# Queries, keys, values and tail contexts of the last attention in four column tiles

## The chip, the cores and the metric

The kernel runs on one core of one Trainium2 chip. The metric is the device time of one execution in microseconds (us). Before the change three runs gave 2605.72, 2614.56 and 2616.25 us; the median is 2614.56. In the profiles, PE is TensorE (matmuls), PEld its loading of the stationary side, DVE is VectorE, ACT is ScalarE, POOL is GpSimd, and SP issues most of the DMAs.

## The reference

Four layers follow each other, each added to its input: a self-attention with 8 heads, a causal convolution, a GRU over 256 steps, and a second attention with 16 heads of 16 channels over 256 channels and 512 positions, for 16 batches. All of it is float32. Only the last one is touched:

```python
def proj(W):
    y = jnp.einsum('oc,bct->bto', W, x)
    return y.reshape(B, T, H, Dh).transpose(0, 2, 1, 3)
Q, K, V = (proj(Wq), proj(Wk), proj(Wv))
att = jnp.einsum('bhqd,bhkd->bhqk', Q, K) * (1.0 / math.sqrt(Dh))
att = att + b[0]
m = mask[:, None, None, :]
att = att * m + (1.0 - m) * NEG_INF
att = jax.nn.softmax(att, axis=-1)
y = jnp.einsum('bhqk,bhkd->bhqd', att, V)
```

The mask is drawn with a chance of about one half, so about half of the 512 positions of a batch are keys that count.

## The kernel before

The program runs the first attention, then the convolution and the recurrence together, then the last attention (`attend_together`, from L1251). This form of the last attention is used when the keys that count fit into 320 places (`ROOM`) in every batch; they do here. The kept rows of a batch are first gathered into a table in DRAM and read back (`send`, `fetch_table`), so that scores and contexts are computed for 320 keys in place of 512: two chunks of 128 and a tail of 64.

**A batch.** `gather` transposes the kept rows (L1323) and the batch's x (L1338) on PE, and makes the values: for each of three key chunks a matmul of the kept rows with the value weights (L1351). `heads` makes queries and keys for half of the heads at a time (L1381). `group` then works on one of four groups; a group takes every other head of one half, four heads, each in 32 of the 128 partitions. It computes scores with queries in the rows for the maximum over keys (L1415 for the two chunks, L1421 for the tail), which DVE takes (L1430, L1435, L1442). The maxima are transposed on PE (L1448) and added to the queries (L1451), so that the second scores (L1461), with keys in the rows, come out shifted; ACT exponentiates them (L1468). `weigh` multiplies these with the values (L1475 for chunks, L1479 for the tail) and adds the chunks in one bank, which ACT copies out (L1488). `finish` sends the sums to DRAM, inverts them on DVE, spreads them, and scales and adds on POOL (L1516 to L1524) before the output goes out.

**Tile shapes on PE.** The profile names a matmul's tile as rows*columns of the array that it occupies. A float32 matmul of the code shows as two MATMUL rows, and each is called a pass here. Steps of this stage come in five shapes: 128*128 (transposes and the products L1351 and L1381); 32*128, four row tiles abreast (L1415, L1461 for the chunks); 64*128, two row tiles (L1421, L1461 for the tail); 128*32, four column tiles abreast (L1475); and 128*64, two column tiles (L1479). The recurrence and its input products (L1063, L1075, L1084) use 128*32 throughout. Passes that run abreast are called a wave.

The tail holds 64 keys, but its score is laid out so that the 128 partitions hold two heads' tail keys each, 64 and 64. The tail's values (`V3`) therefore have zeros for the other head in each half.

**Who sets the order.** The last attention is not written in the order in which it runs. Each step is put into a `Plan` (L168) with an engine, a duration, a due time, what it depends on and which buffers it takes. `Plan.order` then simulates the engines and picks, among the steps that can start, the one that is due first. A step on PE has a mode beside it; a step of the mode that ran last is treated as due 0.25 earlier (`STAY`), and one of another mode is taken to cost 0.2 more (`SWITCH`). Steps without a mode, the transposes and products, count as one mode of their own. The result is a fixed order for each engine, and each engine runs its own in sequence.

Buffers that matter here: three pairs of score banks (`pairs`), one small bank for transposes and products (`banks`), one bank for contexts (`accs`), three for exponentials (`es_`).

Of the kernel before, what the change touches and what calls it, by code (L numbers as in the profile page):

```python
# [16 lines left out]
P = 128  # L17
NEG = -1e30
B, D, T = 16, 256, 512
# [4 lines left out]
H3, DK3, R3 = 16, 16, 32  # L24
# [226 lines left out]
def tile_kernel(ctx: ExitStack, tc: tile.TileContext, x, cond, Wq0, Wo0, W_ih, W_hh, b_ih, b_hh,  # L251
                Wq3, Wk3, Wv3, b3, consts, out, cols):
    nc = tc.nc
# [997 lines left out]
    def attend_together():  # L1251
# [3 lines left out]
        with ExitStack() as es:  # L1255
# [37 lines left out]
            for i in range(2):  # L1293
# [4 lines left out]
                        nc.gpsimd.memset(V3[i][64 * odd : 64 * odd + 64, :, q, odd::2, e : e + 1], 1.0)  # L1298
                nc.gpsimd.memset(NM[i], 0.0)

            def gather(b, g0):

                ub, mk, t, xk, x3, v = us.new(), mks.new(), ts_.new(), xks.new(), x3s.new(), vs.new()
                n = plan.add("DVE", 0.4, g0 - 4, [us.take(ub)], lambda: nc.vector.tensor_scalar(
                    UB[ub.i], cst("iota"), keysT[:, b : b + 1], NEG, ALU.is_ge, ALU.mult))
                for q in range(2):
                    n = plan.add("DVE", 0.4, g0 - 4, [n] + ([mks.take(mk)] if q == 0 else []), lambda q=q: nc.vector.tensor_scalar(
                        MK[mk.i][:, q], UB[ub.i], cst(f"oneC{q}"), top[:, q : q + 1], ALU.mult, ALU.add))
                us.free(ub, n)
                made = n  # L1310
                sent = [plan.add("POOL", 1.2, g0 - 7, ahead[-3:-2], lambda f=f: send(b, f)) for f in range(NT)]
                landed = plan.add("LAG", 2.0, g0 - 7, sent, lambda: None)
                got = []
                for c0 in (0, 2):
                    got.append(plan.add("SP", 3.0, g0 - 6, [landed] + (got or [ts_.take(t)]), lambda c0=c0: fetch_table(b, c0, XS[t.i])))
                moved, turned = [], []
                for kc in range(KC):
                    sm = banks.new()

                    def turn(kc=kc, sm=sm):  # L1320
                        for c in range(NK):
                            r = P if c < 2 else TAILK
                            nc.tensor.transpose(SM[sm.i][:, c * P : c * P + r], XS[t.i][0:r, c, kc * P : (kc + 1) * P], ident[0:r, 0:r])  # L1323
                    m = plan.add("PE", 0.35, g0 - 4.2 + 0.2 * kc, got + [banks.take(sm)] + ([xks.take(xk)] if kc == 0 else moved), turn)
                    c = plan.add("ACT", 0.5, g0 - 4.2, [m],
                                 lambda kc=kc, sm=sm: nc.scalar.copy(XK[xk.i][:, kc, 0:ROOM], SM[sm.i][:, 0:ROOM]))
                    c = plan.add("ACT", 0.3, g0 - 4.2, [c],
                                 lambda kc=kc, sm=sm: nc.scalar.copy(XK[xk.i][:, kc, ROOM:], SM[sm.i][:, 2 * P : ROOM]))
                    banks.free(sm, c)
                    moved.append(c)  # L1330
                ts_.free(t, m)
                ahead.append(m)
                for kc in range(KC):
                    sm = banks.new()

                    def turn(kc=kc, sm=sm):
                        for j in range(NT):
                            nc.tensor.transpose(SM[sm.i][:, j * P : (j + 1) * P], xT[:, j, b, kc * P : (kc + 1) * P], ident)  # L1338
                    m = plan.add("PE", 0.45, g0 - 3.6 + 0.2 * kc, [banks.take(sm)] + ([x3s.take(x3)] if kc == 0 else turned), turn)
                    c = plan.add("DVE", 0.7, g0 - 3.6, [m], lambda kc=kc, sm=sm: nc.vector.tensor_copy(X3[x3.i][:, kc], SM[sm.i]))  # L1340
                    banks.free(sm, c)
                    turned.append(c)
                v_done = []
                for c0 in range(0, NK, 2):
                    sm = banks.new()
                    some = range(c0, min(c0 + 2, NK))

                    def values(some=some, sm=sm, c0=c0):
                        for c in some:
                            for kc in range(KC):  # L1350
                                nc.tensor.matmul(SM[sm.i][:, (c - c0) * D : (c - c0 + 1) * D],  # L1351
                                                 lhsT=XK[xk.i][:, kc, c * P : c * P + P], rhs=wv3T[:, kc],
                                                 start=(kc == 0), stop=(kc == KC - 1))
                    m = plan.add("PE", 0.86 * len(some), g0 - 1.6 + 0.2 * c0, moved + v_done + [banks.take(sm)] + ([] if c0 else [vs.take(v)]), values)
                    for c in some:
                        def spread(c=c, sm=sm, c0=c0):
                            src = SM[sm.i][:, (c - c0) * D : (c - c0 + 1) * D]
                            if c < 2:
                                dst = V[v.i][:, c].rearrange("p (h q) r -> p h (q r)", q=2).rearrange("p h (m i) -> p h m i", i=DK3)
                                nc.scalar.copy(dst[:, :, 0::3], src.rearrange("p (h m i) -> p h m i", m=2, i=DK3))  # L1360
                                return
                            src = src.rearrange("p (m s q i) -> p m s q i", m=2, q=2, i=DK3)
                            for q in range(2):
                                for odd in range(2):
                                    r = slice(64 * odd, 64 * odd + 64)
                                    nc.scalar.copy(V3[v.i][r, :, q, odd::2, DK3 * q : DK3 * q + DK3], src[r, :, odd::2, q])
                        m2 = plan.add("ACT", 0.4 if c < 2 else 1.0, g0 - 1.6, [m], spread)
                        v_done.append(m2)
                    banks.free(sm, m2)
                return mk, xk, x3, v, moved, turned, v_done, made, m  # L1370

            def heads(b, hp, g0, mk, xk, x3, moved, turned, made):
# [3 lines left out]
                for w, x_, X_, deps, name, n, dur in ((wq3T, x3, X3, turned, "q", T, 1.72), (wk3T, xk, XK, moved + [made], "k", ROOM, 1.1)):  # L1376
                    sm = banks.new()

                    def product(w=w, x_=x_, X_=X_, n=n, sm=sm):
                        for kc in range(KC):  # L1380
                            nc.tensor.matmul(SM[sm.i][:, 0:n], lhsT=w[:, kc, hp * P : (hp + 1) * P], rhs=X_[x_.i][:, kc, 0:n],  # L1381
                                             start=(kc == 0), stop=(kc == KC - 1))
                    m = plan.add("PE", dur, gp - 2.6 + 0.1 * (name == "k"), deps + [banks.take(sm)] + [(qs if name == "q" else ks).take(x) for x in (qt if name == "q" else kt)], product)
                    for q in range(2):
                        if name == "q":
                            c = plan.add("ACT", 0.7, gp - 2.6, [m], lambda q=q, sm=sm: nc.scalar.activation(
                                Q[qt[q].i], SM[sm.i], AF.Identity, bias=cst(f"oneC{q}"), scale=cst(f"scaleC{q}")))
                        else:
                            c = plan.add("DVE", 0.6, gp - 2.5, [m], lambda q=q, sm=sm: nc.vector.scalar_tensor_tensor(
                                K[kt[q].i][:, 0:ROOM], SM[sm.i][:, 0:ROOM], cst(f"headC{q}"), MK[mk.i][:, q], ALU.mult, ALU.add))  # L1390
                        done[q].append(c)
                    banks.free(sm, c)
# [10 lines left out]
            def group(g, b, gn, qt, kt, ready, v, v_done):  # L1403
# [50 lines left out]
                for kc in range(NK):  # L1454
# [17 lines left out]
                    def weigh(kc=kc, e=e):  # L1472
                        if kc < 2:
                            for j in range(J):
                                nc.tensor.matmul(AV[acc.i][R * j : R * j + R, :], lhsT=V[v.i][:, kc, 8 * (g // 2) + 2 * j + q],  # L1475
                                                 rhs=E[e.i][:, j], start=(kc == 0), stop=False)
                            return
                        for jp in range(2):
                            nc.tensor.matmul(AV[acc.i][2 * R * jp : 2 * R * jp + 2 * R, :],  # L1479
                                             lhsT=V3[v.i][:, g // 2, q, 2 * jp : 2 * jp + 2].rearrange("p s r -> p (s r)"),  # L1480
                                             rhs=E[e.i][:, jp], start=False, stop=True)
                    last = plan.add("PE", 0.88, gn + kc / NK + 0.2, done + v_done + ([accs.take(acc)] if kc == 0 else [last]), weigh,
                                    mode="c32" if kc < 2 else "c64")
                    es_.free(e, last)
                qs.free(qt, *scored)
                ks.free(kt, *scored)
# [90 lines left out]
```

## Time and profile before

| | us |
|---|---|
| runs before, median (lowest, highest) | 2614.56 (2605.72, 2616.25) |
| the profiled execution | 2617.86 |
| its span | 2616.1 |
| PE busy in the span | 2448.6 |
| DVE busy, ACT busy | 1780.2, 1016.1 |
| L1381 query products, x128 passes of 512 columns, busy | 65.3 |
| L1381 key products, x128 passes of 320 columns, busy | 44.2 |
| L1351 values, x192 passes of 256 columns, busy | 51.8 |
| L1475 contexts of chunks, x1024 passes of 512 columns, busy | 137.2 |
| L1479 contexts of the tail, x256 passes of 512 columns, busy | 69.0 |

The page gives shares of the whole span. The span has three stages with different limits: the first attention up to about 580 us, the recurrence up to about 1680, and the last attention to the end. "Busy" counts the time in which at least one instruction of a group runs, and passes run several abreast, so the busy time of a group divided by its count is not the duration of one. For what a step costs the engine, differences between the starts of neighbouring steps in the timeline are of more use.

### The profile page before, as it was taken

The page shows a single profiled execution, that of the slowest core. Times are in us where ns is not written, and L with a number is a line of the kernel's source. Part 1 is how long each engine was busy: PE and PEld are TensorE (multiplying, and loading weights), DVE is VectorE, ACT ScalarE, POOL GpSimd, SP SyncE. Part 2 cuts the span into 40 slices and gives each one's busy share as a digit, 9 for nine tenths or more (in the row PEclk, how much of TensorE's full clock was granted, in tenths as well). Part 3 has the DMA queues.
Part 4 walks back from the last instruction along what each step waited for, and adds up shares of the span by engine and source line. Part 5 has one row for each costly group of instructions (what it writes and reads, how often), then busy time and mean ns, then how long its engine had stood idle before and what let it go on. Part 6 is the DMA issues. An engine that isn't in the chain of part 4 may idle for free.

```text
span 2616.1 us, 100684 instructions
## 1 busy us (share of the span) xinstructions
PE 2448.6 (94%) x45506; PEld 1635.2 (63%) x45506; DVE 1780.2 (68%) x3810; ACT 1016.1 (39%) x2459; POOL 385.3 (15%) x382
## 2 busy tenths in 40 slices
PE   5999889959999999999999999789999999999995
PEld 3545444437888888888888888644444444444442
DVE  1578778866888888888888655455666566665652
ACT  2444444422333333333333332234444544555452
POOL 2333231210000000000000000132223222231113
PEclk9999999979999999999999999989999999999997
DMA  5222221130000000000000000010011100110001
GB/s 178 69 65 68 62 63 35 35 137 3 5 4 4 5 4 4 4 5 4 4 4 5 5 4 4 5 49 28 28 32 36 41 29 28 33 39 26 19 19 36
DMA packets 54738, 80.22 MB, mean 31 GB/s; under 512 B 15824, under 2 KB 33434, under 8 KB 54292
## 3 DMA queue, kind: packets, MB, share of 16 engines
q1 hardware_dynamic: 45076, 56.66, 7.1%
q0 software_dynamic: 9216, 16.96, 2.2%
q8 instruction: 360, 5.90, 1.0%
q14 instruction: 86, 0.70, 0.1%
HBM read 45.05 MB, written 36.75 MB: 31 GB/s over the span
## 4 chain that ended last, share of the span: by engine, by line
PE 80%; issue 6%; DMA 4%; DVE 4%; POOL 3%; ACT 1%; SPq 0%; POOLq 0%; another core or an unknown queue 0%; DVEq 0%; ACTq 0%
PE pr L1084 10%; PE pz L1084 9%; PE pn L1084 9%; PE sC L1461 8%; PE sC L1415 7%; PE avC L1475 5%; PE pt L1075 4%; PE pr L1063 4%; PE pz L1063 4%; PE smC L1381 4%; PE sC L1421 3%; PE avC L1479 2%; PE smA L908 2%; DMA backA<-result,goto 2%; PE smC L1351 2%
## 5 line engine op out<-in xcount | busy, mean ns | idle before, releaser
L1430 DVE TENSOR_REDUCE nmC<-sC 128x4 f32<-128x1024 f32 x256 | 301.8, 1221 | 208.5 <-PE sC L1415 206.8
L1468 ACT ACTIVATE wih<-sC 128x1024 f32<-128x1024 f32 x320 | 313.6, 1022 | 236.6 <-PE sC L1461 218.6
L1084 PE MATMUL pr<-whh,hist 128*32 128x128 f32 x8192 | 281.6, 275 | 14.2 <-DVE hist L1120 10.2
L1084 PEld LDWEIGHTS pr<-whh,hist 128*32 128x32 f32 x8192 | 218.8, 110 | 118.5 <-DVE hist L1120 51.1
L1084 PE MATMUL pz<-whh,hist 128*32 128x128 f32 x8192 | 279.6, 273 | 2.2 <-issue 2.2
L1084 PE MATMUL pn<-whh,hist 128*32 128x128 f32 x8192 | 278.9, 273 | 0.0
L533 DVE SCALAR_TENSOR_TENSOR yw<-xT,condT,yw 128x512 f32<-128x512 f32 x360 | 269.5, 749 | 6.8
L1063 PE MATMUL pr<-wih,xw 128*32 128x128 f32 x4096 | 222.6, 274 | 22.2 <-DMA wv3nat<-in_L_cond_Wv_dram 19.1
L1084 PEld LDWEIGHTS pz<-whh,hist 128*32 128x32 f32 x8192 | 237.3, 110 | 3.3 <-issue 3.0
L1084 PEld LDWEIGHTS pn<-whh,hist 128*32 128x32 f32 x8192 | 237.1, 110 | 0.1
L1461 PE MATMUL sC<-qC,kC 32*128 32x512 f32 (+1 forms) x1280 | 231.7, 632 | 0.4 <-ACT wih L1468 0.3
L1063 PE MATMUL pz<-wih,xw 128*32 128x128 f32 x4096 | 224.1, 274 | 3.7 <-issue 3.4
L1115 ACT ACTIVATE nn<-pre 128x64 f32<-128x64 f32 x256 | 65.7, 257 | 384.3 <-DVE pre L1113 377.0
L1108 ACT ACTIVATE r<-pr 128x128 f32<-128x128 f32 x256 | 71.0, 277 | 319.2 <-PE pr L1084 318.9
L881 DVE TENSOR_REDUCE whh<-smA 128x2 f32<-128x640 f32 (+2 forms) x211 | 150.2, 752 | 65.1 <-PE smA L873 46.2
L1415 PE MATMUL sC<-kC,qC 32*128 32x256 f32 x2048 | 185.5, 401 | 0.0
L297 POOL DMA_INDIRECT table<-xT,togo x128 | 133.5, 1043 | 248.2 <-DMA table<-xT,togo 169.4
L1516 POOL TENSOR_TENSOR aC<-aC,pbC 128x512 f32<-128x512 f32 x64 | 81.2, 1270 | 590.9 <-ACT wih L1468 287.7
L1075 PE MATMUL pt<-xw,wih 128*32 128x256 f32 x2048 | 166.8, 382 | 0.0
L1288 POOL MEMSET pbC<- 128x512 f32 x4 | 2.3, 625 | 1101.2 <-DVE xT L1092 1101.2
L1109 DVE STREAM_TRANSPOSE rT<-r 128x128 f32<-128x128 f32 x256 | 79.7, 311 | 118.8 <-ACT r L1108 102.4
L1415 PEld LDWEIGHTS sC<-kC,qC 32*128 32x128 f32 x2048 | 128.7, 184 | 46.2 <-issue 16.5
(178 smaller groups left out, 3853.8 us busy)
## 6 DMA issues: line engine op xcount, KB each, us to landing
xA<-in_x_dram SPq DMA_DIRECT2D x16, 512.0 KB
pbC<-sums SPq DMA_DIRECT2D x256, 32.0 KB
out_dram<-oC SPq DMA_DIRECT2D x32, 256.0 KB
table<-zeros SPq DMA_DIRECT2D x16, 320.0 KB
xsA<-table SPq DMA_DIRECT2D x16, 256.0 KB
result<-ocA SPq DMA_DIRECT2D x16, 256.0 KB
xsC<-table SPq DMA_DIRECT2D x16, 256.0 KB
wih<-in_L_cond_W_ih_dram SPq DMA_DIRECT2D x4, 768.0 KB
```

Of the source, the lines that this page charges most:

```text
L297: nc.gpsimd.indirect_dma_start(tables[b], bass.IndirectOffsetOnAxis(togo[:, f, b : b + 1], 0), xT[:, f, b], None, bounds_check=ROOM - 1, o ...
L533: nc.vector.scalar_tensor_tensor(acc, xT[:, f, :, lo : lo + WIN], condT[:, f, k : k + 1], xT[:, f, :, t0 : t0 + WIN] if k == 0 else acc, A ...
L881: nc.vector.tensor_reduce(dst[:, lo : lo + len(some)], SM[0:n, some[0] : some[-1] + 1, 0:ROOM], AX.X, ALU.max, negate=True)
L1063: nc.tensor.matmul(sets[k % 2][0 if g == GATE_R else 2][32 * j : 32 * j + 32].rearrange("p (f i) -> p f i", i=32), lhsT=x2, rhs=gates(wih, ...
L1075: nc.tensor.matmul(ps[32 * j : 32 * j + 32], lhsT=wih[:, kc, 2 * T + fo * P + 32 * j : 2 * T + fo * P + 32 * j + 32], rhs=parts[p][:, kc]. ...
L1084: nc.tensor.matmul(ps[32 * j : 32 * j + 32].rearrange("p (f i) -> p f i", i=32), lhsT=slot[:, f], rhs=gates(whh, f, j)[:, g], start=False, ...
L1381: nc.tensor.matmul(SM[sm.i][:, 0:n], lhsT=w[:, kc, hp * P : (hp + 1) * P], rhs=X_[x_.i][:, kc, 0:n], start=(kc == 0), stop=(kc == KC - 1))
L1415: nc.tensor.matmul(S[st[j // 2].i][:, j % 2, u * 2 * P : (u + 1) * 2 * P], lhsT=Q[qt.i][R * j : R * j + R, c : c + P], rhs=K[kt.i][R * j : ...
L1430: nc.vector.tensor_reduce(dst[:, :, :, e_at + 1], S[st[jp].i].rearrange("p j (u k) -> p j u k", u=2), AX.X, ALU.max, negate=True)
L1461: nc.tensor.matmul(S[st[j // 2].i][:, j % 2, :], lhsT=K[kt.i][r, kc * P : kc * P + P] if kc < 2 else K[kt.i][r, ROOM:], rhs=Q[qt.i][r, :], ...
L1468: lambda jp=jp, st=st, e=e: nc.scalar.activation(E[e.i][:, 2 * jp : 2 * jp + 2], S[st[jp].i], AF.Exp))
L1475: nc.tensor.matmul(AV[acc.i][R * j : R * j + R, :], lhsT=V[v.i][:, kc, 8 * (g // 2) + 2 * j + q], rhs=E[e.i][:, j], start=(kc == 0), stop= ...
```

## The change

Queries, keys and values are computed by four matmuls of 32 columns each in place of one of 128. A helper, `columns`, issues them, all with the same right side. The tail's contexts, so far two matmuls of 64 columns that each served two heads, become four of 32 columns. The plan's modes follow: products, values and tail contexts now carry the mode "c32" of the other contexts. The plan's durations and due times stay.

```diff
+            def columns(ps, left, right, kc):
+
+                for j in range(4):
+                    r = slice(R3 * j, R3 * j + R3)
+                    nc.tensor.matmul(ps[r], lhsT=left[:, r], rhs=right, start=(kc == 0), stop=(kc == KC - 1))
+
             def gather(b, g0):
...
                     def values(some=some, sm=sm, c0=c0):
                         for c in some:
                             for kc in range(KC):
-                                nc.tensor.matmul(SM[sm.i][:, (c - c0) * D : (c - c0 + 1) * D],
-                                                 lhsT=XK[xk.i][:, kc, c * P : c * P + P], rhs=wv3T[:, kc],
-                                                 start=(kc == 0), stop=(kc == KC - 1))
-                    m = plan.add("PE", 0.86 * len(some), g0 - 1.6 + 0.2 * c0, moved + v_done + [banks.take(sm)] + ([] if c0 else [vs.take(v)]), values)
+                                columns(SM[sm.i][:, (c - c0) * D : (c - c0 + 1) * D], XK[xk.i][:, kc, c * P : c * P + P], wv3T[:, kc], kc)
+                    m = plan.add("PE", 0.86 * len(some), g0 - 1.6 + 0.2 * c0, moved + v_done + [banks.take(sm)] + ([] if c0 else [vs.take(v)]), values, mode="c32")
...
                     def product(w=w, x_=x_, X_=X_, n=n, sm=sm):
                         for kc in range(KC):
-                            nc.tensor.matmul(SM[sm.i][:, 0:n], lhsT=w[:, kc, hp * P : (hp + 1) * P], rhs=X_[x_.i][:, kc, 0:n],
-                                             start=(kc == 0), stop=(kc == KC - 1))
-                    m = plan.add("PE", dur, gp - 2.6 + 0.1 * (name == "k"), deps + [banks.take(sm)] + [...], product)
+                            columns(SM[sm.i][:, 0:n], w[:, kc, hp * P : (hp + 1) * P], X_[x_.i][:, kc, 0:n], kc)
+                    m = plan.add("PE", dur, gp - 2.6 + 0.1 * (name == "k"), deps + [banks.take(sm)] + [...], product, mode="c32")
...
-                        for jp in range(2):
-                            nc.tensor.matmul(AV[acc.i][2 * R * jp : 2 * R * jp + 2 * R, :],
-                                             lhsT=V3[v.i][:, g // 2, q, 2 * jp : 2 * jp + 2].rearrange("p s r -> p (s r)"),
-                                             rhs=E[e.i][:, jp], start=False, stop=True)
+                        for j in range(J):
+                            nc.tensor.matmul(AV[acc.i][R * j : R * j + R, :], lhsT=V3[v.i][:, g // 2, q, j],
+                                             rhs=E[e.i][:, j // 2], start=False, stop=True)
                     last = plan.add("PE", 0.88, gn + kc / NK + 0.2, done + v_done + ([accs.take(acc)] if kc == 0 else [last]), weigh,
-                                    mode="c32" if kc < 2 else "c64")
+                                    mode="c32")
```

More of the change, by code (lines that the diff above doesn't have):

```diff
@@ L1380, in product @@
                         for kc in range(KC):
-                            nc.tensor.matmul(SM[sm.i][:, 0:n], lhsT=w[:, kc, hp * P : (hp + 1) * P], rhs=X_[x_.i][:, kc, 0:n],
-                                             start=(kc == 0), stop=(kc == KC - 1))
-                    m = plan.add("PE", dur, gp - 2.6 + 0.1 * (name == "k"), deps + [banks.take(sm)] + [(qs if name == "q" else ks).take(x) for x in (qt if name == "q" else kt)], product)
+                            columns(SM[sm.i][:, 0:n], w[:, kc, hp * P : (hp + 1) * P], X_[x_.i][:, kc, 0:n], kc)
+                    m = plan.add("PE", dur, gp - 2.6 + 0.1 * (name == "k"), deps + [banks.take(sm)] + [(qs if name == "q" else ks).take(x) for x in (qt if name == "q" else kt)], product, mode="c32")
                     for q in range(2):
```

## The prediction

> **What bounds the kernel now.** I read the page first: the busy shares, then the chain that ended last.
>
> ```profile
> PE 2448.6 (94%) x45506; PEld 1635.2 (63%) x45506; DVE 1780.2 (68%) x3810; ACT 1016.1 (39%) x2459; POOL 385.3 (15%) x382
> ...
> PE 80%; issue 6%; DMA 4%; DVE 4%; POOL 3%; ACT 1%; SPq 0%; POOLq 0%; another core or an unknown queue 0%; DVEq 0%; ACTq 0%
> ```
>
> PE is 80% of the chain. An average says nothing about one stage, so next comes the table by stage for the last attention, with one steady batch in it (columns: length, then busy time of each engine with its instruction count).
>
> ```profile
> 1706.00:2590.00 884.00, 873.07 (x6536) 416.26 (x6536) 529.97 (x788) 430.29 (x605) 208.92 (x179) 0.99 0.11 31
> 2030.35:2084.56 54.21, 54.21 (x412) 25.78 (x411) 33.30 (x51) 26.94 (x38) 13.97 (x12) 1.00 0.13 35
> ```
>
> One batch takes 54.2 us; PE is shown busy for all of it, DVE for 33 and ACT for 27. But a busy PE is not a PE at its peak, so I looked at the timeline of PE inside that batch (start, length, line, count) and took differences of starts.
>
> ```profile
> 2030.29 1.99 PE L1381 MATMUL smC<-whh,wq3T 128*128 128x512 f32 x4
> 2032.20 1.08 PE L1479 MATMUL avC<-wih,whh 128*64 128x512 f32 x4
> 2033.21 1.14 PE L1461 MATMUL sC<-qC,kC 32*128 32x512 f32 x8
> 2034.28 1.34 PE L1381 MATMUL smC<-xkC,wk3T 128*128 128x320 f32 x4
> 2035.55 1.14 PE L1461 MATMUL sC<-qC,kC 32*128 32x512 f32 x8
> 2036.62 1.06 PE L1475 MATMUL avC<-wih,whh 128*32 128x512 f32 x8
> 2037.62 0.66 PE L1448 MATMUL smC<-C,nmC 128*128 128x128 f32 x4
> ...
> 2066.00 1.99 PE L1351 MATMUL smC<-wv3T,xkC 128*128 128x256 f32 x8
> 2067.92 1.14 PE L1461 MATMUL sC<-qC,kC 32*128 32x512 f32 x8
> ```
>
> The query product (four passes of 512 columns) takes 32.20 - 30.29 = 1.91, the key product (four of 320) 35.55 - 34.28 = 1.27. The difference, 0.64 us for 4 x 192 columns, is 0.833 ns per column and pass. So the query's array time is 4 x 512 x 0.833 = 1.71 and the key's 1.07: each spends 0.205 on something else. Two column-tiled contexts (L1475, eight passes, four abreast, so two waves of 512) take 37.62 - 36.62 = 1.00, array time 0.853: 0.145 beside it. The tail's context in two halves (L1479) takes 1.01: 0.155. I call this the entry and exit of a tile shape: what PE pays when one step's shape follows another's. That it is a price of changing shape is shown where shapes don't change. In the recurrence, all of it 128*32:
>
> ```profile
> 1178.21 0.43 PE L1063 MATMUL pr<-wih,xw 128*32 128x128 f32 x8
> 1178.42 0.43 PE L1063 MATMUL pz<-wih,xw 128*32 128x128 f32 x8
> 1178.64 0.43 PE L1063 MATMUL pr<-wih,xw 128*32 128x128 f32 x8
> 1178.86 0.43 PE L1063 MATMUL pz<-wih,xw 128*32 128x128 f32 x8
> 1179.08 0.64 PE L1075 MATMUL pt<-xw,wih 128*32 128x256 f32 x8
> ```
>
> Groups of two waves of 128 columns start every 0.217 us; 256 x 0.833 ns is 0.213. New weights, another target bank, even another width next (L1075), and nothing is lost.
>
> **The change, part by part.** No arithmetic is taken away. It does two things: the shape of 96 product steps and 64 tail contexts becomes 128*32, and the planner, told so, lays PE's steps in another order. SP, ACT and POOL issue the same instructions in the same order as before, every DMA and queue included; DVE has one tail maximum (L1435) and one mask (L1307) moved per batch.
>
> *Array time.* Columns: four matmuls of 32 columns abreast stream the same right side, so the query product is four waves of 512 instead of four passes of 512: 1.71 either way. The same holds for keys, values and tail contexts (two halves by 512 twice, or two waves of 512). Change: 0. The nearest row is L1075 in the recurrence, which has exactly this form (four left sides, one right side). A rule of the Trainium skill speaks against it: TensorE: Matmul & The Clock Gate, section "Measured speedup vs the span model", gives three column tiles of width 32 a speedup of 2.38, which is 79% of three. If the products ran at 79%, their array time, 32 x 1.71 + 32 x 1.07 + 16 x (1.71 + 0.85) = 130 us, would become 164: +34. By the row it is +2% at most (0.217 to 0.213), +2. I take the row: it is this chip in this kernel, with groups that follow each other, and I put that 2 into the range.
>
> *Entry and exit of an isolated product.* Today 0.205 for each of 96 steps (L1381 and L1351; 0.21 for 2067.92 - 2066.00 less 1.71). A column-tiled step pays 0.14, by L1475, the only row of the new shape between other shapes in this stage. 96 x 0.065 = 6.2 us less. From both sides: nothing, if loading the same weights costs what it cost; 0.065 if the narrower loads (108 ns against 190 in the rows of this stage) shorten the entry as they do in L1475. I take the row, 6.2.
>
> *Tail contexts.* 0.155 to 0.14: 64 x 0.013 = 0.8 us less.
>
> *Changes of shape that go.* This I counted in the two built PE orders of the last attention, 800 steps each. Neighbours that are both 128*32: 1 before, 98 after (context and tail; context, query, tail; context, key, tail). Each saves one exit and one entry, 0.14: 97 x 0.14 = 13.6 us. Two full-shape neighbours that need no change today, 9, are only 4 after (products next to transposes, in the first batch): 5 x 0.16 = 0.8 lost. A 128*32 step directly ahead of a 32-row score stands 123 times in the new order and never in this trace; the neighbours of it that do stand (128*32 ahead of 64 rows or of a full shape, 1.00; 128*64 ahead of 32 rows, 1.01) bound it between 0.14 and 0.155, at most 1.6 us worse. I take 0.14.
>
> Sum of PE's own time: -6.2 - 0.8 - 13.6 + 0.8 = -19.8 us, in a steady batch about -1.26 of 54.2.
>
> *What waiting gives back.* PE also waits in a batch, about 2.9 us at seven places, always for one of the three pairs of score banks: a score step, its exponential on ACT, then the pair is free. I read these from the timeline of all engines.
>
> ```profile
> 2043.50 1.13 PE L1461 MATMUL sC<-qC,kC 64*128 64x512 f32 x4
> 2044.56 0.66 PE L1338 MATMUL smC<-C,xT 128*128 128x128 f32 x4
> 2044.75 1.02 ACT L1468 ACTIVATE wih<-sC 128x1024 f32<-128x1024 f32 x1 [1.65 <-PE sC L1461]
> 2045.14 1.81 PE L1461 MATMUL sC<-qC,kC 32*128 32x512 f32 x8
> 2045.82 0.30 PEld L1461 LDWEIGHTS sC<-qC,kC 32*128 32x128 f32 x4 [0.38 <-ACT wih L1468]
> ```
>
> The 64-row score starts at 2043.50; its pair comes back at 2045.82, 2.32 later (score to exponential 1.25, the exponential 1.02, 0.05 until PE goes on). Meanwhile PE had the transpose of x (L1338, 0.59), and so waited 0.68 in the middle of the next score. In the new order this transpose stands ahead of the 64-row score: score follows score directly (7 such places before, 20 after, so one more in 13 batches). The cover of 0.59 is gone, and the wait becomes 0.68 + 0.59. Queued behind it on PE are the transpose of the maxima (L1448), on which DVE's shift of the queries waits, and the next maxima. Two smaller ones: the second values step stands before a score half that waits already (0.12 at 2070.05), so its 0.065 is waited instead; and the key product stands between two exponential scores whose pair is just in time, about 0.04. Together 0.69 a batch, 13 x 0.69 = 9.0 us. The ends: 0, if other steps slide into the gap; all of the 19.8, if every saving ends before a wait of this sort. I take 9, because the other five waits stand where the new order keeps the same steps between the score and the reuse of its pair.
>
> *Other costs.* PE gets some 1,600 more matmuls and as many loads (queries, keys, values 448 to 1,792, tails 256 to 512): issue is no limit, since in this stage PE would run 8,136 in 873 us, 9 per us, against 24,576 + 8,192 + 2,048 in the recurrence's 1,040, over 30. The end after PE's last context (2585 to 2616: sums, reciprocal, spreads, output) has the same instructions in the same order: 0.
>
> Sum: -19.8 + 9.0 = -10.8 us. The profiled execution took 2617.86 (span 2616.1, 1.8 around it), so it would take 2607.1; that execution lies 3.3 above the median of 2614.56, and the median would be **2603.8**, 0.41% less. A measurement of this kernel can tell about 0.5% from no change, 13.1 us, so the forecast lies just inside "same": 2601.5 is the border.
>
> **Rivals.** *B, the switches go and no wait grows:* 2614.6 - 19.8 = 2594.8. For it: ACT and DVE are idle 40 to 50% of a batch, and runs of before reach down to 2605.7. Against it: the three pairs and their order are fixed, and in that order nothing stands between the two scores.
>
> *C, waits eat nearly all:* PE runs ahead, and the pairs' turnaround sets the batch. Then some 2 us stay: 2612. For it: seven waits a batch today. Against it: of these only two stand behind a step that gets shorter or loses its cover, and one wait is new.
>
> *D, slower:* four column tiles that share one right side don't run four abreast behind row-tiled scores, L1381 and L1351 alone. By the rule above +34, less 10.8: 2638. Slower by 0.5% begins where (13.1 + 10.8) / 130 = 18% is added, 505 ns for a 512-column wave. The recurrence's rows speak against it plainly.
>
> *E, the change does nothing* can't be: the built orders differ.
>
> **How the numbers follow.** A (the forecast) 0.55, its own range 2598 to 2608; B 0.25; C 0.12; D 0.08. A third of A lies under 2601.5, with all of B: faster 0.18 + 0.25 = 0.43. Same: the rest of A and C, 0.49. Slower 0.08. The range reaches from B's 2595 less 2 to C's 2612 plus 1: 2593 to 2613.
>
> **What would show it.** Right: L1381 and L1351's successors at 128*32, x16 for a query in 1.71 to 1.85 instead of 1.91, a key in 1.07 to 1.21, contexts and tail at 0.87 to 1.00 each, in one run without gaps; a batch of 53.6; a wait of about 1.25 where the 64-row score of the exponentials is followed by the next score. Wrong: a wave of 512 over 430 ns in a product; a gap of 0.14 between two 128*32 steps; PE waits a batch far from 3.6; an end after PE's last context that isn't 31.

## The result and the profile after

The changed kernel takes 2605.32 us in the median, the kernel before 2613.69 in the runs beside it; the medians differ by 8.4 us, 0.32%. The ratio, taken over all runs but one, is 0.9962 with a 95% interval of 0.9953 to 0.9970: 0.38% or 7.8 to 12.3 us faster, where 0.41% (10.8 us, to 2603.8) was forecast. That is inside the 0.5% called "same", but the interval leaves no room for "no change". One of the 22 runs of the changed kernel took 7947.25 us, three times the others, for a reason that nothing here shows; it is left out of the ratio.

The two profiled executions differ by more: their spans are 2616.1 and 2597.2. Of these 18.9 us only 12 belong to the stage that was changed. The last attention's first matmul on PE starts at 1683.25 before and at 1675.83 after, and up to there both programs issue the same work. In the ten profiles of this study that start lies between 1673.37 and 1683.25, and the profile before is the latest of them. So totals are compared over many runs below, and a profile is read by its stage alone: from the first transpose of the last attention on PE to the start of the last context copy on ACT. That stage is 902.3 us before and 890.4 after. Within it, the batches of either profile agree within 0.4 us, but for the first and the last two, where work starts or runs out.

The page after, busy time and chain:

```profile
PE 2431.5 (94%) x47106; PEld 1606.1 (62%) x47106; DVE 1782.3 (69%) x3810; ACT 1016.6 (39%) x2459; POOL 386.3 (15%) x382
...
PE 76%; issue 6%; DVE 4%; DMA 3%; POOL 3%; ACT 1%; SPq 0%; POOLq 0%; DVEq 0%; ACTq 0%
```

PE has the 1,600 more matmuls, is busy for 17 us less, and still leads the chain. The table by stage, before and after, and one steady batch after (length; busy time of PE, PEld, DVE, ACT and POOL; granted clock, DMA share, GB/s):

```profile
1683.25:2586.14 902.89, 882.23 (x6560) 420.22 (x6560) 539.36 (x804) 433.38 (x610) 221.25 (x204) 0.99 0.11 31
...
1675.83:2566.78 890.95, 866.44 (x8160) 395.50 (x8160) 541.72 (x804) 434.76 (x610) 220.83 (x204) 0.98 0.11 31
...
2018.08:2071.65 53.57, 52.84 (x514) 23.92 (x510) 33.90 (x51) 27.05 (x38) 13.88 (x13) 1.00 0.12 34
```

(A stage's row reaches to the end of the copy, 0.6 us further.) A batch takes 53.57, forecast 53.6. The timeline of PE in it answers to that shown of before. The helper `columns` gives queries, keys and values one line, L1305; a context of a chunk is now L1478, one of the tail L1482, and an exponential score L1464.

```profile
2017.20 1.06 PE L1478 MATMUL avC<-wih,whh 128*32 128x512 f32 x8
2018.08 1.90 PE L1305 MATMUL smC<-whh,wq3T 128*32 128x512 f32 x16
2019.80 1.04 PE L1482 MATMUL avC<-wih,whh 128*32 128x512 f32 x8
2020.77 1.14 PE L1464 MATMUL sC<-qC,kC 32*128 32x512 f32 x8
2021.84 1.28 PE L1305 MATMUL smC<-xkC,wk3T 128*32 128x320 f32 x16
2023.06 1.15 PE L1464 MATMUL sC<-qC,kC 32*128 32x512 f32 x8
...
2053.46 1.93 PE L1305 MATMUL smC<-wv3T,xkC 128*32 128x256 f32 x32
2055.32 1.14 PE L1464 MATMUL sC<-qC,kC 32*128 32x512 f32 x8
```

By the differences of starts: the context ahead of the query takes 0.88 (1.00 before), the query itself 1.72 for an array time of 1.71, the tail context 0.97. Together the three take 3.57 for an array time of 3.41: 0.16 beside it, hardly more than the 0.145 of one such step alone. Three steps of one shape run through with one entry and one exit between them. The key product, alone between scores, takes 1.22 (1.27 before), the two value chunks 1.86 (1.92).

A cover is here the work on PE that fills the time until a pair of score banks comes free. Where it went, in the timeline of all engines:

```profile
2030.86 0.66 PE L1344 MATMUL smC<-C,xT 128*128 128x128 f32 x4
2031.44 0.30 PEld L1464 LDWEIGHTS sC<-qC,kC 64*128 64x128 f32 x4 [0.17 <-issue]
2031.44 3.41 PE L1464 MATMUL sC<-qC,kC 64*128 64x512 f32 x12
2032.50 0.30 PEld L1464 LDWEIGHTS sC<-qC,kC 32*128 32x128 f32 x4 [0.76 <-DVE nmC L1433]
2032.65 2.10 ACT L1471 ACTIVATE wih<-sC 128x1024 f32<-128x1024 f32 x2 [3.25 <-PE sC L1464]
2033.72 0.30 PEld L1464 LDWEIGHTS sC<-qC,kC 32*128 32x128 f32 x4 [0.92 <-ACT wih L1471]
```

The transpose of x (L1344) now stands ahead of the 64-row score. The next score starts right behind it, at 2032.50, and its second half at 2033.72: 1.22 us apart, where they were 0.68 apart before. PE's row hides this: x12 in one piece of 3.41 us, all of it "busy". Nor does PE stand still in most of that time: until 2033.63 it runs the first half, two of the four row tiles. What is lost is that the second half would otherwise run beside it; a whole score of 32 rows takes 1.07 where it waits for nothing (2034.28 - 2033.21 in the profile before).

### The profile page after: what moved, and what is told of

The parts are those of the page before. It is cut to its first block, busy times and chain, and to the rows that moved or that the text cites. A ratio compares the mean times of both kernels' runs of the same rounds, so it can differ in the third digit from the quotient of the medians.

```text
span 2597.2 us, 103897 instructions
## 1 busy us (share of the span) xinstructions
PE 2431.5 (94%) x47106; PEld 1606.1 (62%) x47106; DVE 1782.3 (69%) x3810; ACT 1016.6 (39%) x2459; POOL 386.3 (15%) x382
## 4 chain that ended last, share of the span: by engine, by line
PE 76%; issue 6%; DVE 4%; DMA 3%; POOL 3%; ACT 1%; SPq 0%; POOLq 0%; DVEq 0%; ACTq 0%
PE pr L1084 10%; PE pz L1084 9%; PE pn L1084 9%; PE sC L1464 7%; PE sC L1418 7%; PE smC L1305 5%; PE avC L1478 5%; PE pt L1075 4%; PE pr L1063 4%; PE pz L1063 4%; PE sC L1424 3%; PE avC L1482 2%; PE smC L1451 1%; DMA backA<-result,goto 1%; PE smA L908 1%
## 5 line engine op out<-in xcount | busy, mean ns | idle before, releaser
L1464 PE MATMUL sC<-qC,kC 32*128 32x512 f32 (+1 forms) x1280 | 237.4, 632 | 1.3 <-ACT wih L1471 0.3
```

The source lines that it names most:

```text
L1464: nc.tensor.matmul(S[st[j // 2].i][:, j % 2, :], lhsT=K[kt.i][r, kc * P : kc * P + P] if kc < 2 else K[kt.i][r, ROOM:], rhs=Q[qt.i][r, :], ...
```

## Experiments

Shape and order are two things here, and the sum of the prediction kept them apart: the shapes' prices (-19.8) and the waits of the new order (+9.0). So the first four kernels take them apart in the program. Stage and total of each stand in one table behind the last.

**The new shapes in the old order.** The planner isn't told of them. Against the changed kernel, cut:

```diff
-  ... + ([] if c0 else [vs.take(v)]), values, mode="c32")
+  ... + ([] if c0 else [vs.take(v)]), values)
-  ... for x in (qt if name == "q" else kt)], product, mode="c32")
+  ... for x in (qt if name == "q" else kt)], product)
-                                    mode="c32")
+                                    mode="c32" if kc < 2 else "c64")
```

> The new shapes (products, values and tail contexts as 128*32) in the PE order of the kernel before: the planner is told nothing of them. The stage is measured from the first transpose of the last attention on PE to the last copy of a context on ACT: 902.3 us before, 890.4 after. Theory (entry and exit of shapes, less what the new order gives back in waits): in the old order 85 neighbours become 128*32, so 84 x 0.14 + 96 x 0.065 + 64 x 0.013 = 18.8 less, up to 9 x 0.16 = 1.4 lost at full-shape neighbours, and the transpose stays between the 64-row score and the next: waits grow by 1 only. Stage 902.3 - 16.5 = 885.8 (+-2), faster than the change itself; a batch 53.15. Rival 'the planner's grouping is what gains': stage 902. Rival 'narrow products are cheaper, neighbours don't matter': 902.3 - 7 = 895.

Measured: stage 886.0, a batch 53.15; the total is 0.9931 of before (0.9905 to 0.9957). The stage falls by 16.3, forecast 16.5: the shapes pay, and they pay more where the order stays. The stage's row:

```profile
1673.37:2559.97 886.60, 863.24 (x8160) 395.49 (x8160) 540.19 (x804) 433.54 (x610) 221.06 (x204) 0.99 0.10 32
```

**The old shapes in the new order.** Modes as in the changed kernel, matmuls as in the one before. Against the changed kernel, cut:

```diff
-                                columns(SM[sm.i][...], XK[xk.i][:, kc, c * P : c * P + P], wv3T[:, kc], kc)
+                                nc.tensor.matmul(SM[sm.i][...], lhsT=XK[xk.i][:, kc, c * P : c * P + P], rhs=wv3T[:, kc], ...)
-                            columns(SM[sm.i][:, 0:n], w[:, kc, hp * P : (hp + 1) * P], X_[x_.i][:, kc, 0:n], kc)
+                            nc.tensor.matmul(SM[sm.i][:, 0:n], lhsT=w[:, kc, hp * P : (hp + 1) * P], rhs=X_[x_.i][:, kc, 0:n], ...)
-                        for j in range(J):   # tail contexts, 32 columns each
+                        for jp in range(2):  # 64 columns each
```

> The old shapes (products and values 128*128, tail contexts 128*64) in the PE order of the changed kernel. Theory: no price of a shape is saved and the wait behind the uncovered 64-row score grows by 0.59 a batch: stage 902.3 + 7.6 = 909.9 (+-2), a batch 54.75, slower than before. Rival 'the planner's grouping is what gains': stage 890 to 892. Rival 'waits don't depend on the order': 902.

Measured: stage 910.1, a batch 54.7; the total is 1.0024 of before (1.0008 to 1.0040). So the planner's new order alone makes the kernel slower, by 7.8 us of stage. Its timeline has the two scores in one piece of 3.41 us, though its shapes are the old ones:

```profile
2038.77 0.66 PE L1344 MATMUL smC<-C,xT 128*128 128x128 f32 x4
2039.35 3.41 PE L1467 MATMUL sC<-qC,kC 64*128 64x512 f32 x12
```

**Products alone, and tail contexts alone,** each with its mode told to the planner:

> Queries, keys and values in four column tiles with their mode told to the planner; tail contexts in two tiles of 64 columns as before. Theory: 33 neighbours of 128*32, 32 x 0.14 + 96 x 0.065 = 10.7 less, waits +1: stage 902.3 - 8.6 = 893.7 (+-2), a batch 53.6. Rival 'each part gains for itself': products 12 less, since they are most of the array time: 890.5.

> Only the tail contexts in four column tiles, with their mode; products as before. Theory: 36 neighbours, 35 x 0.14 + 64 x 0.013 = 5.7 less, but the planner now moves the tail's maximum scores and the transpose of x, the cover of the 64-row score goes, waits grow by 7.5: stage 902.3 + 1.9 = 904.2 (+-2), a batch 54.4, not faster than before. Rival 'each part gains for itself': stage 902.3 - 5.7 = 896.6.

Measured: stages 893.4 and 903.8. The products give 8.9 of the stage and the tail takes 1.5 (its total can't be told from no change); together they give 11.9. The parts don't add up, as neighbours of one shape need both of their sides: the traces have 33 and 36 of them alone and 98 together, and the 29 more at 0.14 are 4.1 of the 4.5 us that are missing. That the tail alone loses has another reason. It is the tail's mode that moves the 64-row maximum score in the planner's order, and the lost cover comes with it: a 64-row score of the exponentials is followed at once by the next score in 20 places with the tail alone, and in 7, as before, with the products alone.

**The cover put back.** One number is added to the changed kernel (the line is cut):

```diff
-  m = plan.add("PE", 0.9, gn - LEADS + part / 3, ready + ...
+  m = plan.add("PE", 0.9, gn - LEADS + part / 3 - 0.3 * (part == 2), ready + ...
```

> The changed kernel with one number more: the tail's maximum scores are due 0.3 earlier, so that in the planner's order the transpose of x stands between the 64-row score of the exponentials and the next score again, as it did before the change. Shapes and modes are those of the changed kernel, 83 neighbours of 128*32 are left (98 without this number). Theory (the wait of 0.59 a batch comes from that lost cover): the stage, from the first transpose to the last context copy, falls from 890.4 to 885.7 (+-1.5), a batch from 53.56 to 53.14; the idle time in front of that score's second half goes from about 1.3 back to 0.7. Rival 'the wait is the narrow shapes' own, whatever stands between': 890, or 892 with 15 neighbours fewer.

Measured: stage 886.1, a batch 53.2, total 0.9936 of before (0.9923 to 0.9950). In its timeline the transpose is back between the scores, and the halves start at 2032.26 and 2032.94, 0.68 apart as before:

```profile
2030.62 1.13 PE L1464 MATMUL sC<-qC,kC 64*128 64x512 f32 x4
2031.68 0.66 PE L1344 MATMUL smC<-C,xT 128*128 128x128 f32 x4
2032.26 0.30 PEld L1464 LDWEIGHTS sC<-qC,kC 32*128 32x128 f32 x4 [0.17 <-issue]
2032.27 1.81 PE L1464 MATMUL sC<-qC,kC 32*128 32x512 f32 x8
2032.94 0.30 PEld L1464 LDWEIGHTS sC<-qC,kC 32*128 32x128 f32 x4 [0.38 <-ACT wih L1471]
```

A due time on one kind of step is worth 4.3 us of stage, with nothing changed in the work. That is net of a loss: in this order 83 neighbours of 128*32 are left of the 98.

**Other due times.** If waits for score pairs are what is left, an order with more steps between a score and its pair's next use should take them away. Two kernels try this. `SLACK` is how far behind the earliest possible start the planner still looks for the step that is due first (0.12 so far). The second kernel has, against the changed kernel (lines cut, remarks added):

```diff
+            plan.SLACK, plan.STAY = 0.45, 0.3
-  m = plan.add("PE", 0.35, g0 - 4.2 + 0.2 * kc, got + ...                    # transposes of kept rows
+  m = plan.add("PE", 0.35, g0 - 4.0 + 0.2 * kc, got + ...
-  m = plan.add("PE", 0.86 * len(some), g0 - 1.6 + 0.2 * c0, moved + ...       # values
+  m = plan.add("PE", 0.86 * len(some), g0 - 1.6 + 0.2 * (c0 or 1), moved + ...
-  m = plan.add("PE", dur, gp - 2.6 + 0.1 * (name == "k"), deps + ...          # queries, keys
+  m = plan.add("PE", dur, gp - 2.6 - 0.8 * (name == "k"), deps + ...
-  m = plan.add("PE", 0.9, gn - LEADS + part / 3, ready + ...                  # scores for the maximum
+  m = plan.add("PE", 0.9, gn - LEADS + part / 3 - 0.3 * (part < 2), ready + ...
-  m = plan.add("PE", 0.88, gn + kc / NK, [shifted] + ...                      # scores for the exponential
+  m = plan.add("PE", 0.88, gn + kc / NK - 0.4 * (kc < 2), [shifted] + ...
-  last = plan.add("PE", 0.88, gn + kc / NK + 0.2, done + ...                  # contexts
+  last = plan.add("PE", 0.88, gn + kc / NK + 0.8, done + ...
```

The first has `SLACK` 0.45 and `STAY` 0.5, both kinds of 32-row scores due 0.6 earlier and the contexts 0.6 later (the 0.8 in the cut), and leaves the rest.

> The changed kernel with other numbers for the planner: scores of 32 rows due 0.6 earlier, contexts 0.6 later, of the steps that can start within 0.45 (0.12) the first due is taken, and a step of the same mode counts 0.5 (0.25) earlier. Work is the same. If waits for the three score pairs are what is left beside the prices of shapes, an order that keeps more steps between a score and the reuse of its pair takes most of them away: waits fall by some 40 of 80 us, and 40 neighbours of 128*32 are lost (+5.5). Stage 857 (+-5), total about 2570. Rival 'the pairs' turnaround is fixed by ACT and DVE': stage 885 or more, since PE has nothing else to run.

> As the last, with key products due 0.9 earlier, values and the transposes of kept rows 0.2 later, same mode 0.3 earlier, maximum scores 0.3 and exponential scores 0.4 earlier. Theory: waits fall by 50 us; stage 848 (+-6), total about 2561. Rival: as before, 885.

Measured: stages 855.9 and 851.6; totals 0.9822 (0.9809 to 0.9834) and 0.9815 (0.9803 to 0.9828) of before. The two can't be told apart by their totals; both are far faster than the kernel before and the changed one. In the second, waits fall by 2.7 us a batch against the change, 43 over 16 batches, while 62 neighbours of 128*32 are lost (36 are left), some 9 us at 0.14: by this estimate 34 of the 38.8 us by which its stage is shorter. The stage of the second:

```profile
1677.91:2530.14 852.23, 831.92 (x8160) 368.94 (x8160) 565.28 (x804) 431.06 (x610) 221.76 (x204) 0.98 0.10 33
```

DVE and ACT do the same number of instructions in 39 us less: their work did not set the stage, nor do they now (565 and 431 of 852).

**The same due times with the old shapes and modes:**

> The same numbers for the planner with the old shapes and the old modes (products 128*128, tail contexts 128*64). Theory: most of the gain of due times is in waits and comes here as well: stage 902.3 - 34.8 = 867.5 (+-5); the shapes' own part in this order is the rest, 19. Rival 'due times gain only through more neighbours of one shape': stage 900, as none are there.

Measured: stage 875.2, total 0.9915 (0.9902 to 0.9928). Most of the due times' gain, 27 us, comes without the new shapes, as expected, but 7.7 us less of it than was expected, outside the range given. The two kernels with these due times lie 23.5 us apart, not 19, and not by their shapes alone: the modes differ too, and with them the planner's order. Worked out by step from the two traces, beside array time, the queries, keys, values and contexts hold 11 of the 23.5, close to the 12 that the prices above give for them (96 x 0.065 + 64 x 0.013 + 35 x 0.14). The other 12 are in the 64-row scores, whose shape is the same in both. With the new modes two of these scores mostly follow each other (60 such neighbours in the stage):

```profile
2013.70 1.13 PE L1465 MATMUL sC<-qC,kC 64*128 64x512 f32 x4
2014.67 1.06 PE L1425 MATMUL sC<-kC,qC 64*128 64x128 f32 x16
2015.65 1.07 PE L1306 MATMUL smC<-wv3T,xkC 128*32 128x256 f32 x16
```

With the old modes many stand apart (33 neighbours are left), and each then takes longer for the same array time of 0.85: the exponential score 1.06 in place of 0.97, the maximum score 1.10 in place of 0.98.

```profile
2029.05 1.13 PE L1468 MATMUL sC<-qC,kC 64*128 64x512 f32 x4
2030.11 0.64 PE L1330 MATMUL smC<-C,xsC 128*128 128x128 f32 x3
...
2032.77 1.16 PE L1428 MATMUL sC<-kC,qC 64*128 64x128 f32 x16
2033.87 0.64 PE L1330 MATMUL smC<-C,xsC 128*128 128x128 f32 x3
```

The 27 neighbours that are gone make some 5 us at this price; no run separates the rest.

| kernel | stage, us | total against before | waits in a batch, us |
|---|---|---|---|
| before | 902.3 | 1 | 2.9 |
| the change | 890.4 | 0.9962 (0.9953 to 0.9970) | 3.5 |
| shapes, old order | 886.0 | 0.9931 (0.9905 to 0.9957) | 3.0 |
| order, old shapes | 910.1 | 1.0024 (1.0008 to 1.0040) | 3.5 |
| products only | 893.4 | 0.9979 (0.9969 to 0.9989) | 3.0 |
| tail only | 903.8 | 1.0003 (0.9994 to 1.0013) | 3.5 |
| the change, cover put back | 886.1 | 0.9936 (0.9923 to 0.9950) | 3.0 |
| the change, due times | 855.9 | 0.9822 (0.9809 to 0.9834) | 1.3 |
| the change, more due times | 851.6 | 0.9815 (0.9803 to 0.9828) | 0.8 |
| old shapes, those due times | 875.2 | 0.9915 (0.9902 to 0.9928) | 0.8 to 1.1 |

The last column is worked out, not read: over eight steady batches, the differences of PE's starts less array time (0.833 ns per column and wave) and less the entry and exit of each step's shape as measured where nothing is waited for. It is good to 0.1 or 0.2; in the last row it hangs on which price the 64-row scores are given. Each total is set against runs of the kernel before made beside it.

## Why the prediction was right, point by point

*Array time, 0.* Right. A query product in four column tiles takes 1.72 with neighbours of its shape, for 1.71 in the array; the 34 us that the prediction estimated from the speedup of three column tiles in the Trainium skill (TensorE: Matmul & The Clock Gate, "Measured speedup vs the span model") are not there. The two values chunks, eight waves of 256, take 1.86.

*Entry and exit, -6.2, -0.8 and -13.6.* Right in sum. The new shapes in the old order test these prices with hardly any change of waits, and gave 16.3 for 16.5. Singly they are not quite as put. In a run of neighbours, all but one step were put at their bare array time and that one at 0.14 more; context, query and tail pay 0.03, 0.01 and 0.12. A product alone was put at 0.14 beside its array time and pays 0.15 (keys 1.22 less 1.07, values 1.86 less 1.71). 128*32 ahead of 32 rows, never seen before, was taken at 0.14 and bounded by 0.14 and 0.155: the products' 0.15 lies at the upper bound, and the 0.12 of a tail context at the end of a run (0.97 less 0.85) outside. In the sum they matter little: less its waits, a batch fell from 51.3 to 50.07, 1.23 for the 1.26 forecast.

*Waits, +9.0.* The mechanism is shown. The second half of the next score starts 1.22 after the first (1.27 forecast, 0.68 before); the old shapes in the new order get slower by 7.8 (7.6 forecast); the cover put back takes 4.3 off the stage (4.7 forecast). Waits in a batch went from 2.9 to 3.5, 0.6 for the 0.69 forecast, and nearly all of it, 0.54, at the uncovered place. The other waits kept their sum, about 2.3 a batch, but not each its place: one of 0.65 in a maximum score now lies in part or whole at the exponential score ahead of it.

*The sum, -10.8.* The stage fell by 11.9, a batch by 0.6. The 1.1 between them is within what the waits were put too high: 13 x 0.69 was 9.0, and 13 x 0.6 is 8. The total can't tell as much: its interval, 7.8 to 12.3 us, would hold any sum near these, and that the median of 2605.32 lies 1.5 from the forecast is in part luck, since single runs of one kernel scatter over 9 us and more.

*The end after PE, 0.* Right: the span ends 30.5 us after the last copy starts before, 31.0 after.

*The rivals.* B, no wait grows, is refuted for the change, but not as a possibility: with one due time more the waits are nearly those of before (3.0), and the total of 0.9936 (0.9923 to 0.9950) reaches B's 0.9924. C, waits eat nearly all, is refuted by the stage's 11.9. D, no four abreast behind row-tiled scores, is refuted by the query's 1.72 and by the key's 1.22 right behind a score of 32 rows.

What the prediction did not see is how much stood beside it. It took the five other waits as given, "because the other five waits stand where the new order keeps the same steps". That holds for this order, in their sum; the due times show that most of these waits were the order's own: 3.5 us a batch became 0.8 with the same shapes, and 2.9 became about 1 with the old ones.

## What to carry to other kernels

Where an engine's busy time fills its stage, take differences of starts: what they held here beyond array time was the price of changing shape and hidden waits, and each was shortened with no work removed. A change of shape that also goes through a planner is two changes; run the shape in the old order and the order with the old shape, since here the one gave 16 us and the other took 8. When steps move, look at what stood between a producer and the next use of its buffer, for that cover is what is lost.

## What was not expected of the hardware

The time until the last attention starts differs between the profiled executions by up to 9.9 us (1673.37 to 1683.25) for the same work, while the steady batches of the last attention, before and after, agree within 0.4 us and the stages of the first five experiments came within 0.4 us of what was worked out for them. That scatter is as large as the effect measured here, and the stage read from one profile told more than a handful of timed runs. What in the earlier stages makes it was not looked into.

The prices of shapes came out the same to 0.01 us nearly everywhere that a step stood between the same two neighbours and waited for nothing, in every order tried: 0.142 to 0.143 for a context between scores, 0.208 to 0.209 for a 128*128 product, 0.148 to 0.149 for a product in four column tiles.
